# Sparse graph attention on 16 graphs: a longer lead of the later projections, two products held back, and no output product in the last places

## The chip, the cores and the metric

The kernel runs on one core of a Trainium2 chip. The metric is the device time of one execution in microseconds (us), the median of several runs. Engines are called PE (TensorE matmul; PEld is its weight load), DVE (VectorE), ACT (ScalarE), POOL (GpSimd) and SP (SyncE, which here only issues DMAs).

## The reference

The input x is 16 batches of 1024 nodes with 512 features (float32), adj a 1024 x 1024 matrix of zeros and ones that all batches share; it is sparse, with few ones in most rows and many in the first ones. There are 8 heads of 64 features.

```python
q = (x @ Wq + bq).reshape(b, n, H, HD)        # k, v alike
scores = jnp.einsum('bqhd,bkhd->bhqk', q, k) / jnp.sqrt(jnp.float32(HD))
scores = scores + (1.0 - adj)[None, None, :, :] * -1000000000.0
attn = jax.nn.softmax(scores, axis=-1)
out = jnp.einsum('bhqk,bkhd->bqhd', attn, v).reshape(b, n, d)
layer = out @ Wo + bo
x = _layernorm(x + layer, axis=-1, eps=1e-5)
```

A row of adj without any one attends to all nodes alike, so its result is the mean of v.

## The kernel before, in words

**Data.** The nodes are sorted by degree, and a batch's rows form 8 tiles of 128 queries (NT = 8). Because a query has only a few keys, attention is no dense matmul: for each tile the kernel walks over *blocks*, and a block holds one key for each of the tile's 128 queries. POOL gathers the key and value rows of a block by an indirect DMA (`kvg`, L1242) from a DRAM buffer `kv_pair`, which holds k and v of two batches (the first two batches have buffers of their own, `kv_rows`; PAIRED_FROM = 2). DVE multiplies q by k (`qk`, L1263) and reduces by head (`s`, L1267); ACT takes exponentials (L1278) and weighs v with them (L1291), or DVE does (L1295); DVE adds two weighed blocks (L1307); PE sums them in PSUM (`sum`, L1316 and L1317). After a tile's last block DVE normalises it (`o`, L1329 to L1337), and PE transposes it (`poT`, L1351) for its output product `po` with Wo (L790). A statistic chain over DVE, ACT and POOL (L1100 to L1125; the power at L1113 or L1143 on POOL, the shift at L1116 on DVE) makes the layer norm, and POOL stores the rows (L1125).

**The order of the work.** All engines' instructions are written out in one order (manual schedule). A loop counts *places* n, from -39 to some 540. There are 530 blocks, one per place; batch b begins at place `start[b]`: 0, 34, 68, 100, 134, 166, 200, 232, 266, 298, 332, 364, 398, 430, 464, 496, and 530 is the end. At place n the loop writes the products and scores of block n+4, exponentials of n+3, weighing of n+1 or n+2, the gather of block n+8 (AHEAD; AHEAD_LAST = 11 once no projections are left), and callbacks that earlier places left for this one (`later(k, fn)`: k places on). Then it lets PE do *units* as long as a *credit* lasts, which grows by a share per place: pieces of output products (`finish`, four matmul units and, late in the run, one for the bias), or the next unit of `fronts`, a list with the projections of the batches to come. A function put into `urgent` goes as well (the transposes `turn`, and `mean_pe`).

**Fronts.** For each pair of tiles (`pair`) these are: the transposes of x (`transpose_x`, pxT L748), q (pq, L790), and k and v by seven half products (x, p*, z; L947) that DVE and ACT combine (L959 to L980). Each tile's `out` callback starts the load of x three tiles on (`load_x`, for batches above 0 an indirect DMA of POOL, L1001; three buffers), and for tiles in STORED also a store of x as residual (SP). k and v go to DRAM through SP (L840), q as well; after the last pair PE makes the mean of v (pm, L858), whose write (L864) sets `set_up[b]`; only then may gathers of batch b be written. The first gather of an odd batch from 3 on is `more` (L1217): the first tile of two successive batches is worked off together in the odd one.

How many fronts are done in batch b's stretch is set by a lead in places ahead of a batch's start: `ahead = EARLY + FIRST * (1 - max(0, b - 1) / LATE)`, with EARLY = 13, FIRST = 11 and LATE = 12. In the last batches (from 13 on) the share spreads what is left over the places up to `fronts_end`.

**The lead-in.** Before place 0 the kernel also builds the key lists from adj. Those of tile 7 and 6 are built beside the first places (`REST_FROM`), by a generator `edges(t)`: each `yield` in it means one place later. DVE finds the sorted keys (L635 to L669), PE counts the degrees before each query (`poff`, L675), DVE goes on (L677 to L688, `codes`), PE places them (`pe` L698, `pof` L719), and DVE extracts. Another generator, `bias_setup`, makes the bias of the output: PE transposes the bias rows (L408), DVE copies and spreads bv (`bvb`, L415), PE multiplies by Wo (`pb`, L419), DVE adds bo (L421).

**The end.** After the last projection, output products are the only units of PE beside the sums. `finishing` holds the units of the product begun; none is begun in the last two places of 530. Products of some tiles (SPILL) have their transposed inputs stored and are reloaded (`reload`) for this end, named oTs in the profile.

Of the kernel before, what the change touches and what calls it, by code (L numbers as in the profile page):

```python
# [38 lines left out]
PAIRED_FROM, SPARED = 2, 56  # L39
# [9 lines left out]
AHEAD_LAST = 11  # L49

ROWS = 3
EARLY = 13

FIRST = 11
LEAD_IN = 39
FRONT_BY = -14
SEGMENT = 64
# [120 lines left out]
def kernel(  # L178
# [37 lines left out]
    B, N, D = x.shape  # L216
    HD = D // HEADS
    NPAIR = D // P
    NT = N // P
# [28 lines left out]
    def broadcast(t, v):  # L248
        nc.scalar.dma_start(t, bass.AP(tensor=v.tensor, offset=v.offset, ap=[[0, P], [1, D]]))
# [4 lines left out]
    with ExitStack() as main:  # L254
# [6 lines left out]
        def fill_psum(name):  # L261
            return psum.tile([P, HALF], F32, tag="fill", name=name, bufs=4)
# [74 lines left out]
        def merged(b):  # L337
            return b >= PAIRED_FROM and b % 2 == 1
# [55 lines left out]
        def bias_setup():  # L394
            bk_bc = work.tile([P, D], F32, tag="y", name="bk_bc", bufs=Y_BUFS)
            broadcast(bk_bc, bk)
            yield
            n4 = small.tile([P, NPAIR], F32, name="bk_norms", bufs=1)
            nc.vector.tensor_tensor(bk_bc, bk_bc, bk_bc, op=OP.mult)
            nc.vector.tensor_reduce(n4, bk_bc.rearrange("p (h d) -> p h d", d=P), axis=AX.X, op=OP.add)  # L400
            nc.vector.tensor_reduce(bk_norm, n4, axis=AX.X, op=OP.max)
            n8 = small.tile([P, HEADS], F32, name="bq_norms", bufs=1)
            nc.vector.tensor_tensor(bk_bc, bq_bc, bq_bc, op=OP.mult)
            nc.vector.tensor_reduce(n8, bk_bc.rearrange("p (h d) -> p h d", d=HD), axis=AX.X, op=OP.add)
            nc.vector.tensor_reduce(bq_norm, n8, axis=AX.X, op=OP.max)
            yield
            pb = fill_psum("pb")
            nc.tensor.transpose(pb[:, 0:2 * NPAIR], bias_rows, ident[:2 * NPAIR, :2 * NPAIR])  # L408
            nc.tensor.transpose(pb[:, 2 * NPAIR:3 * NPAIR], bv_rows, ident[:NPAIR, :NPAIR])
            yield  # L410
            nc.vector.tensor_copy(bias_qk, pb[:, 0:2 * NPAIR])
            bv_col = one.tile([P, NPAIR], F32, name="bv_col")
            nc.vector.tensor_copy(bv_col, pb[:, 2 * NPAIR:3 * NPAIR])
            bvb = work.tile([P, NPAIR, P], F32, tag="y", name="bvb", bufs=Y_BUFS)
            nc.vector.tensor_copy(bvb, bv_col[:, :, None].to_broadcast([P, NPAIR, P]))  # L415
            yield
            pb = fill_psum("pb3")
            for c in range(NPAIR):
                nc.tensor.matmul(pb, bvb[:, c, :], W["o"][:, c, :], start=(c == 0), stop=(c == NPAIR - 1))  # L419
            yield  # L420
            nc.vector.tensor_tensor(bo_bc, pb, bo_bc, op=OP.add)  # L421
# [18 lines left out]
        now, plan, rest, urgent, known, waiting, combined = [0], {}, {}, [], [], [], []  # L440

        def later(k, fn):
            plan.setdefault(now[0] + k, []).append(fn)
# [187 lines left out]
        def edges(t):  # L631
# [38 lines left out]
                nc.vector.tensor_tensor(check[:, 2 * NT + 1:2 * NT + 2], ranked[:, t, 1:2], st[:, 0:1], op=OP.subtract)  # L670

            nc.vector.tensor_scalar(deg, ranked[:, t, 1:2], -float(K), 0.0, op0=OP.add, op1=OP.max)
            yield
            po = fill_psum(f"poff_{t}")
            nc.tensor.matmul(po[:, 0:1], before, deg, start=True, stop=True)  # L675
            yield
# [15 lines left out]
            for i0 in range(0, nb, step):  # L692
                n = min(step, nb - i0)
# [21 lines left out]
            for i0 in range(0, nb, 4):  # L715
                n = min(4, nb - i0)
# [15 lines left out]
        def load_x(b, t):  # L732
            if b < B:
                if b and not known:
                    waiting.append((b, t))
                    return
                X[b, t] = work.tile([P, D], F32, tag="x", name=f"x_{b}_{t}", bufs=3)
                if b:
                    gather_x(X[b, t], b, t)
                else:  # L740
                    nc.sync.dma_start(X[b, t], x[b, ds(t * P, P), :])

        def transpose_x(b, t):
            def pe():
                xs = X.pop((b, t))
                p = fill_psum(f"pxT_{b}_{t}")
                for c in range(NPAIR):
                    nc.tensor.transpose(p[:, ts(c, P)], xs[:, ts(c, P)], ident)  # L748

                def out():  # L750
                    XT[b, t] = work.tile([P, D], F32, tag="xT", name=f"xT_{b}_{t}", bufs=4)
                    nc.scalar.copy(XT[b, t], p)
                    n = b * NT + t + 3
                    if t == 0 and b >= PAIRED_FROM:
                        if not merged(b):
                            BOTH[b // 2] = work.tile([P, 2, NPAIR, P], F32, tag="place", name=f"both_{b}", bufs=1)
                        nc.scalar.copy(
                            BOTH[b // 2].rearrange("p w c (h n) -> p h c w n", h=2)[:, b % 2],
                            p.rearrange("p (c w n) -> p c w n", c=NPAIR, w=2),
                        )  # L760
                        sq = work.tile([P, D], F32, tag="ysq", name=f"sq_x_{b}", bufs=1)
                        nc.scalar.activation(sq[0:LONE, :], xs[0:LONE, :], AF.Square, accum_out=x_norm[0:LONE, b:b + 1])
                    if b * NT + t in STORED:
                        nc.sync.dma_start(residual[b * NT + t], xs)
                        later(2, lambda: load_x(n // NT, n % NT))
                    else:
                        load_x(n // NT, n % NT)
                    if t % 2 and (b, t) != (0, 1):
                        later(1, combine)

                def combine():
                    s = [work.tile([P, HD2], F32, tag=f"s{i}", name=f"s{i}_{b}_{t}", bufs=1 + i // 4) for i in (1, 2, 3, 4)]
                    x0, x1 = XT[b, t - 1], XT[b, t]
                    nc.vector.tensor_tensor(s[0], x1[:, 0:HD2], x1[:, HD2:D], op=OP.add)
                    nc.vector.tensor_tensor(s[2], x0[:, 0:HD2], x1[:, 0:HD2], op=OP.subtract)
                    nc.vector.tensor_tensor(s[1], s[0], x0[:, 0:HD2], op=OP.subtract)
                    nc.vector.tensor_tensor(s[3], x0[:, HD2:D], s[1], op=OP.subtract)
                    SX[b, t // 2] = s

                later(1, out)  # L780

            return [(TRANSPOSE, pe, lambda: (b, t) in X)]
# [403 lines left out]
        start = [min(n for n, block in enumerate(blocks) if block[0] == b) for b in range(B)] + [len(blocks)]  # L1186
# [245 lines left out]
        done, coming, spilled, gathered, fronts, guarded = [], [], [], [0], [], []  # L1432

        total = len(blocks)
# [19 lines left out]
        for t, n in REST_FROM.items():  # L1454
            prep.setdefault(n, []).append(edges(t))
# [7 lines left out]
        with tc.manual_schedule():  # L1463
# [13 lines left out]
                return fronts_by[b - 1] + (part - int(part)) * (fronts_by[b] - fronts_by[b - 1])  # L1477

            finishing, last_finish, reloads, last_reload = [], -LEAD_IN, 0, 0
            fronts_end = start[B - 1] - 12  # L1480
            credit = 0.0
            for t in range(3):
                load_x(0, t)
            n = -LEAD_IN
            while n < total or plan or rest or urgent or done or finishing or spilled or lone_tiles or not guarded:
# [6 lines left out]
                elif n in start:  # L1492

                    b = start.index(n)
                    left = sum(u[0] for u in fronts)
                    ahead = EARLY + FIRST * (1 - max(0, b - 1) / LATE)
                    goal = fronts_time - needed(b + 2, ahead / NBT)
# [38 lines left out]
                    reload(*spilled.pop(0), reloads)  # L1536
                    reloads, last_reload = reloads + 1, n
                first_unit = True
                while credit > 0 or urgent:
                    if urgent and not (first_unit and fronts):  # L1540
                        urgent.pop(0)()
                        continue
                    if (
                        not finishing and len(done) > (LAZY if fronts else 0) and n > loaded.get(done[0], n) + 1
                        and n > last_finish + bool(fronts) and not total - 2 <= n < total
                    ):
                        finishing = finish(*done.pop(0))
                        last_finish = n
                    units = finishing or fronts
                    if not units:  # L1550
                        if urgent:
                            urgent.pop(0)()
                            continue
                        break
                    cost, fn, ready = units[0]
                    if ready and not ready():
                        if urgent:
                            urgent.pop(0)()
                            continue
                        break  # L1560
                    del units[0]
                    fn()
                    credit -= cost
                    first_unit = False
                credit = min(credit, 2 * share)
# [39 lines left out]
```

## Time and profile before

| What | us |
| --- | --- |
| median of three runs | 1888.14 |
| the three runs | 1887.98, 1894.98, 1888.14 |
| the profiled execution | 1894.52 |
| its span, first to last instruction | 1892.4 |
| PE busy in it, mean granted clock 0.990 | 1816.5 |
| first score reduction (L1267) of batch 12, 13, 14, 15 | 1436.00, 1535.97, 1636.63, 1746.03 |

The profile is one execution; its span is 2.1 us shorter than its time, and its time is 6.4 us above the median. A place takes about 3.1 us (2.96 in batch 13, 3.46 in batch 15). Units of PE by the groups: one matmul of 128x512 about 0.6 us in the records, and as each is pipelined with the next, two of them (the two passes of a float32 product) take 0.86 us of PE in sequence. The groups with the most DVE time are the reduction of scores (681 ns each), the product with q (684 ns) and the addition of two blocks (694 ns); a gather on POOL takes 1131 ns.

### The profile page before, as it was taken

The page shows a single profiled execution, that of the slowest core. Times are in us where ns is not written, and L with a number is a line of the kernel's source. Part 1 is how long each engine was busy: PE and PEld are TensorE (multiplying, and loading weights), DVE is VectorE, ACT ScalarE, POOL GpSimd, SP SyncE. Part 2 cuts the span into 40 slices and gives each one's busy share as a digit, 9 for nine tenths or more (in the row PEclk, how much of TensorE's full clock was granted, in tenths as well). Part 3 has the DMA queues.
Part 4 walks back from the last instruction along what each step waited for, and adds up shares of the span by engine and source line. Part 5 has one row for each costly group of instructions (what it writes and reads, how often), then busy time and mean ns, then how long its engine had stood idle before and what let it go on. Part 6 is the DMA issues. An engine that isn't in the chain of part 4 may idle for free. (4 is left out here: it accounts for less than half of the span.)

```text
span 1892.4 us, 25171 instructions
## 1 busy us (share of the span) xinstructions
PE 1816.5 (96%) x5149; PEld 876.6 (46%) x5149; DVE 1695.3 (90%) x3470; ACT 1557.4 (82%) x6128; POOL 1262.6 (67%) x1189
## 2 busy tenths in 40 slices
PE   7979999999999999999999999999999999999996
PEld 3434444444545454444444444444545444444442
DVE  6888879999998999899999989899999989997875
ACT  3627868988888988988898878988899989977885
POOL 1366765777676776767676766767676866656884
PEclk9989999999999999999999999999999999999998
DMA  7356786888989897989889897989889899989993
GB/s 279 115 167 215 226 290 229 309 298 291 322 266 319 303 333 256 345 290 310 299 284 329 279 324 261 334 303 309 286 302 352 297 332 319 329 282 319 340 332 137
DMA packets 188149, 544.63 MB, mean 288 GB/s; under 512 B 32602, under 2 KB 32622, under 8 KB 187986
## 3 DMA queue, kind: packets, MB, share of 16 engines
q0 software_dynamic: 116400, 382.82, 60.4%
q1 hardware_dynamic: 68510, 154.30, 21.7%
q10 hardware_dynamic: 3076, 5.82, 0.8%
q14 instruction: 120, 0.98, 0.2%
q8 instruction: 43, 0.70, 0.2%
HBM read 419.52 MB, written 144.34 MB: 298 GB/s over the span
## 5 line engine op out<-in xcount | busy, mean ns | idle before, releaser
L1291 ACT ACTIVATE pv<-kvg,pv 128x64 f32<-128x64 f32 x3544 | 893.4, 340 | 1.8 <-issue 1.8
L1242 POOL DMA_INDIRECT kvg<-kv_pair,place_row x462 | 522.6, 1131 | 258.6 <-issue 94.5
L790 PE MATMUL po<-wo,oT 128*128 128x512 f32 x816 | 379.2, 600 | 2.0 <-DVE vsum L854 1.2
L790 PE MATMUL pq<-wq,xT 128*128 128x512 f32 x792 | 369.4, 598 | 1.3 <-DVE s L1267 0.8
L1267 DVE TENSOR_REDUCE s<-qk 128x8 f32<-128x512 f32 x530 | 360.8, 681 | 7.2
L1263 DVE TENSOR_TENSOR qk<-qt,kvg 128x512 f32<-128x512 f32 x434 | 296.8, 684 | 13.2 <-DMA kvg<-kv_pair,place_row 13.1
L947 PE MATMUL x<-b,xT 128*128 128x512 f32 x504 | 239.0, 597 | 0.1
L947 PE MATMUL pp<-t,s 128*128 128x512 f32 x504 | 237.3, 593 | 1.5 <-DVE t L383 1.5
L1307 DVE TENSOR_TENSOR pv<-pv,pv 128x520 f32<-128x520 f32 x329 | 228.4, 694 | 8.2 <-ACT pv L1291 8.0
L790 PEld LDWEIGHTS po<-wo,oT 128*128 128x128 f32 x816 | 153.4, 192 | 171.7 <-issue 162.7
L790 PEld LDWEIGHTS pq<-wq,xT 128*128 128x128 f32 x792 | 149.0, 192 | 169.3 <-issue 157.7
L1001 POOL DMA_INDIRECT x<-in_x_dram,asked_row x120 | 129.6, 1080 | 103.5 <-PE pxT L748 35.4
L1278 ACT ACTIVATE pv<-s,absent 128x8 f32<-128x8 f32 x434 | 126.8, 293 | 55.1 <-DVE s L1267 36.6
L1125 POOL DMA_INDIRECT out_dram<-y,asked_row x129 | 145.1, 1125 | 35.9 <-issue 25.0
L800 ACT ACTIVATE sq_k<-kv 128x128 bf16<-128x128 f32 x512 | 150.8, 300 | 8.4 <-DVE kv L970 4.5
L947 PEld LDWEIGHTS x<-b,xT 128*128 128x128 f32 x504 | 95.3, 192 | 111.6 <-issue 105.2
L947 PEld LDWEIGHTS pp<-t,s 128*128 128x128 f32 x504 | 94.1, 190 | 111.3 <-issue 102.2
L947 PE MATMUL z<-b,s 128*128 128x512 f32 x252 | 121.4, 604 | 13.1 <-DVE kv L975 10.4
L1196 POOL DMA_INDIRECT qg<-q_rows,query_row x96 | 105.5, 1099 | 28.5 <-issue 25.3
L1029 POOL DMA_INDIRECT y<-in_x_dram,asked_row x93 | 105.0, 1129 | 26.1 <-issue 25.8
L947 PE MATMUL z<-t,s 128*128 128x512 f32 x252 | 118.6, 593 | 0.0
L947 PE MATMUL pp<-t,xT 128*128 128x512 f32 x252 | 118.5, 592 | 0.0
(276 smaller groups left out, 2750.2 us busy)
## 6 DMA issues: line engine op xcount, KB each, us to landing
kv_pair<-kv SPq DMA_DIRECT2D x98, 512.0 KB
q_rows<-q SPq DMA_DIRECT2D x106, 256.0 KB
qt<-q_rows SPq DMA_DIRECT2D x98, 256.0 KB
residual<-x SPq DMA_DIRECT2D x36, 256.0 KB
y<-residual SPq DMA_DIRECT2D x36, 256.0 KB
kv_rows<-kv SPq DMA_DIRECT2D x15, 512.0 KB
kvg<-kv_pair,place_row POOLq DMA_INDIRECT x462
kv_pair<-kv SPq DMA_DIRECT2D x28, 256.0 KB
```

The lines of the kernel that those rows point to most:

```text
L790: nc.tensor.matmul(p, lhs(c), w[:, c, :], start=(c == 0), stop=(c == NPAIR - 1))
L800: nc.scalar.activation(sq, s[:, ts(h, P)], AF.Square, scale=scale, accum_out=sums[:, h:h + 1])
L947: nc.tensor.matmul(R[bank], l[:, ts(c, P)], right[:, c, :], start=(first and c == 0), stop=(c == 1), skip_group_check=True,)
L1001: nc.gpsimd.indirect_dma_start(out=y, out_offset=None, in_=x_rows, in_offset=bass.IndirectOffsetOnAxis(ap=asked_row[:, t:t + 1], axis=0), ...
L1125: nc.gpsimd.indirect_dma_start(out=out_rows[b, t], out_offset=bass.IndirectOffsetOnAxis(ap=rows, axis=0), in_=y, in_offset=None, element_o ...
L1196: nc.gpsimd.indirect_dma_start(out=q, out_offset=None, in_=q_rows[b % ROWS], in_offset=bass.IndirectOffsetOnAxis(ap=rows, axis=0))
L1242: nc.gpsimd.indirect_dma_start(out=KG[n], out_offset=None, in_=rows, in_offset=bass.IndirectOffsetOnAxis(ap=(place_row if b else key_row)[ ...
L1263: nc.vector.tensor_tensor(QK[n], q, KG[n][:, 0:D], op=OP.mult)
L1267: nc.vector.tensor_reduce(S[n], QK.pop(n).rearrange("p (h d) -> p h d", d=HD), axis=AX.X, op=OP.add)
L1278: nc.scalar.activation(PV[n][:, D:], S.pop(n), AF.Exp, bias=bias)
L1291: nc.scalar.activation(pv[:, ts(h, HD)], v[:, ds(D + h * HD, HD)], AF.Copy, scale=pv[:, D + h:D + h + 1])
L1307: nc.vector.tensor_tensor(PV[b, t], PV[b, t], pv, op=OP.add)
```

## The change

It has four parts, all in the order of the work; no instruction is added to or taken from a projection, an attention block or an output product.

- **Held back:** in `edges` and in `bias_setup`, three yields instead of one stand ahead of the products poff and pb, so these are written two places later.
- **Lead:** EARLY becomes 17 and FIRST 7 (their sum stays 24), and `fronts_end` is 16 places ahead of the last batch's start instead of 12.
- **Loads of x:** the load that a tile's `out` starts comes 4 places later instead of 2 for tiles in STORED, and 2 places later instead of at once for the first tile of batches from PAIRED_FROM on.
- **Last places:** in places 527, 528 and 529 no unit of an output product or projection is written; before, only the beginning of a product was excluded, in the places 528 and 529.

```diff
-EARLY = 13
-FIRST = 11
+EARLY = 17
+FIRST = 7
...
             nc.vector.tensor_copy(bvb, bv_col[:, :, None].to_broadcast([P, NPAIR, P]))
-            yield
+            for _ in range(3):
+                yield
             pb = fill_psum("pb3")
...
             nc.vector.tensor_scalar(deg, ranked[:, t, 1:2], -float(K), 0.0, op0=OP.add, op1=OP.max)
-            yield
+            for _ in range(3):
+                yield
             po = fill_psum(f"poff_{t}")
...
                     if b * NT + t in STORED:
                         nc.sync.dma_start(residual[b * NT + t], xs)
+                        later(4, lambda: load_x(n // NT, n % NT))
+                    elif t == 0 and b >= PAIRED_FROM:
                         later(2, lambda: load_x(n // NT, n % NT))
                     else:
                         load_x(n // NT, n % NT)
...
-            fronts_end = start[B - 1] - 12
+            fronts_end = start[B - 1] - 16
...
-                while credit > 0 or urgent:
+                last_sums = total - 3 <= n < total
+                while credit > 0 and not last_sums or urgent:
...
-                    units = finishing or fronts
+                    units = [] if last_sums else finishing or fronts
```

## The prediction

> **What bounds the kernel now.** I read the page's first part (busy time of each engine), then the groups with what ended the idle time before them, then the timeline of PE and DVE around each place that the diff touches, and last the table of windows. The chain of waits helps less: PE has only 28% of it, in pieces of many lines.
>
> ```profile
> PE 1816.5 (96%) x5149; PEld 876.6 (46%) x5149; DVE 1695.3 (90%) x3470; ACT 1557.4 (82%) x6128; POOL 1262.6 (67%) x1189
> ```
>
> PE is busy for 1816.5 of 1892.4 us, so all its idle time is 75.9 us. DVE stands close behind at 90%. No edit takes a matmul away, so the change can win only out of those 75.9 us and out of stretches where PE runs at half clock. From the timeline: the lead-in (the first 160 us) holds the larger waits (7.42, 2.19, 1.20, and the first loads, which no edit touches); from 160 to 1740 us there are some 31 us in 28 small waits; the rest is the tail.
>
> ```profile
> 108.23 0.38 PE L675 MATMUL poff<-est,before 128*128 128x1 f32 x2 [2.19 <-DVE est L669]
> 109.75 1.86 PE L858 MATMUL pm<-vsum,mean 128*1 128x512 f32 x2
> ...
> 136.40 5.44 PE L419 MATMUL pb<-wo,bvb 128*128 128x512 f32 x8 [7.42 <-DVE bvb L415]
> ...
> 157.25 1.98 PE L947 MATMUL z<-b,s 128*128 128x512 f32 x4 [1.20 <-DVE kv L975]
> ```
>
> The columns are start, duration, engine, line, operation; the bracket is the idle time before and its releaser. These are the two products whose yields the diff lengthens: the list offsets (poff) waited 2.19 us and the bias product (pb) 7.42 us, each for a DVE result that DVE had just been given.
>
> At the other end of the run, batch 13 begins at about 1536 us:
>
> ```profile
> 1526.75 1.96 POOL L1217 DMA_INDIRECT more<-kv_pair,place_row  x1 [4.95 <-issue]
> ...
> 1538.72 0.69 DVE L1263 TENSOR_TENSOR qk<-qt,kvg 128x512 f32<-128x512 f32 x1 [1.47 <-DMA kvg<-kv_pair,place_row]
> 1543.34 0.69 DVE L1263 TENSOR_TENSOR qk<-qt,kvg 128x512 f32<-128x512 f32 x1 [1.53 <-DMA kvg<-kv_pair,place_row]
> ...
> 1558.81 0.66 PE L1351 MATMUL poT<-ident,o 128*128 128x128 f32 x4 [1.63 <-DVE o L1337]
> 1565.36 0.66 PE L1351 MATMUL poT<-ident,o 128*128 128x128 f32 x4 [2.46 <-DVE o L1337]
> ```
>
> POOL's first gather of the batch stood 4.95 us before it could start, the gathers behind it came late, DVE waited 1.47 and 1.53 us for them, and PE then waited for DVE.
>
> ```profile
> 109.20:112.60 3.40, 3.40 (x5) 0.63 (x5) 3.30 (x13) 0.57 (x1) 0.00 (x0) 0.50 0.56 189
> 136.40:139.90 3.50, 3.50 (x4) 1.51 (x5) 3.43 (x7) 1.21 (x5) 2.89 (x3) 0.50 0.51 164
> 1535.97:1636.63 100.66, 93.33 (x270) 44.65 (x269) 94.27 (x180) 89.93 (x372) 66.13 (x62) 0.98 0.90 311
> 1846.00:1869.30 23.30, 21.42 (x56) 10.51 (x54) 18.53 (x53) 19.50 (x60) 14.37 (x16) 0.93 0.53 187
> ```
>
> Columns: window, length, busy time (count) of PE, PEld, DVE, ACT and POOL, granted clock, DMA share, GB/s. After the 2.19 and the 7.42 us waits PE ran 3.4 to 3.5 us at clock 0.50. Batch 13's 34 blocks took 100.66 us, of which PE worked 93.33 and DVE 94.27.
>
> **What the skill says of it.** The Trainium skill, "TensorE: Matmul & The Clock Gate", section "Part 1: The HAM clock gate", says that an idle TensorE falls to half clock, judged over windows of about 3.4 us, and advises against gaps of over about 3 us. The trace has the half clock for about that long, but after waits from 1.73 us on, and none after 1.63 us or less. I go by the trace: a wait of 1.7 us or more costs 3.4 / 2 = 1.7 us on top. The same skill's "DMA: Bandwidth & Descriptors", section "Rules for kernel authors", says that a DMA which reads what another wrote has to be held until that one's completion semaphore. The trace agrees: the held gather (4.95 us) reads kv_pair, whose last writes SP issued from 1522.68 to 1527.24. An earlier write is therefore the right lever there.
>
> **The change part by part.** The profiled execution took 1894.52 us (span 1892.4), 6.38 above the median of 1888.14. I sum against 1894.52 and then take 6.38 off.
>
> *A: three yields instead of one ahead of poff and pb.* The instruction order shows no new instruction; products move two places back. For the list of tile 7, PE's next instruction is then pq (no wait, two units), then pm, which needs vsum: DVE finishes that at 109.62, in order behind est, where pm now starts at 109.75. So the 2.19 us just move to pm: gain 0. DVE now waits for pp before g some 4.55 instead of 2.67 us, and its 2.1 us of list work (L677 to L688) go behind g. So DVE finishes bvb at about 137.9 instead of 136.15. PE meanwhile does six units that stood behind pb (two each of pq, x, pp, 6 x 0.86 = 5.2 us, from 128.8 to 133.95), and waits 137.9 - 133.95 = 4.0 instead of 7.42. That still costs the half clock, as before. DVE then sets the pace: transposes wait for a bank (about 1.3), poff for g (about 1.7), and z behind kv (L975) begins at 154.4 instead of 157.25: -2.85. The list's other products now come 0.35 later: **-2.5**. Bounds: -9 if nearly all of both waits goes (2.19 + 7.42 = 9.6), +1 if DVE's added wait of 1.9 us is passed on.
>
> *B: the lead.* With EARLY 17 and FIRST 7 the lead of the projections (13 + 11 places at batches 0 and 1, both 24 in sum) falls more slowly: for b = 12 it is 17 + 7/12 = 17.6 instead of 13.9 places, and the last projection is due at place 480 instead of 484. The instruction order has the batch's last mean (pm) at 14 places ahead of its start instead of 10 (batch 13), 9 (14 and 15); the gathers still run 8 ahead. Four places at 3 us are 12 us, over the 4.95, so POOL's wait goes. The writes of k and v move on SP's queue past some four q reads of 0.3 us (L1229), which have their places of slack; cost 0. What it cost: DVE 1.47 + 1.53 + 0.43 and 2.24 for a statistic of POOL's behind the same queue, 5.7 in sum; PE 0.66 + 1.63 + 2.46 = 4.75, with a half clock 6.4. DVE works 94.27 of the 100.66 us there, so at most 6.4 can go; I take 5. Batch 15's first gather also waited (2.86), but PE has some 3.8 us of work per place there and hides it: 0. Next late: the x of batch 14, tile 5 is loaded one place before its transpose (three or more elsewhere; four in the middle of the run before); a gather of 1.1 us and its landing within some 3 us: 0 to 3 us and a half clock, I take 1.5. Sum **-3.5** (bounds -6.4 and 0). Projections done earlier also leave output products for later; as PE does both, this is a swap, cost 0 while PE is bound.
>
> *C: loads of x two places later (also the first tile of each batch from 2 on).* One POOL DMA each (1.08 us, L1001), moved, none added. In the order each x still has three places or more but the one above. The moved gathers pass kvg gathers on POOL's queue, which is 67% busy; SP's stores keep their places. **0**, with -6 to +6 for the small waits of mid-run, whose order shifts by a few places: some 20 us of them come from PE and DVE handing over, and nothing here takes that away.
>
> *D: no product in places 527 to 529.* In the order the four products that stood behind place 522 (4 x 3.65 = 14.6 us) come before it: the last is at 521 instead of 527, since B's earlier projections also leave places for them. PE's end then: the sums and products up to the last sum ended at 1869.30; without the four sums of 522 to 528 (4 x 0.86) the last product ends at 1865.9, less the idle that it fills: 1.88 and its half clock 1.7 at 1849.40, and half of 4.0 (1.15 + 1.13 + 0.82 + 0.90, PE's waits from 1730 to 1824): 5.6, so 1860.3. Behind it DVE has y (0.7), the four 0.61 us operations of place 523 (2.45), two of 524 with statistics (1.6), four of 525 (2.45) and two of y (1.3); ACT weighs 529 (1.9) behind that, done at about +10; add, sum, and the four operations to o end at +12.7: 1873.0. Before, o was ready at 1871.66. **+1** (bounds -3 and +5: 12.7 may be 10 if ACT hides, or 2.5 more if a statistic waits for POOL). What follows (the last tile's transposes, product, norm, store) is the same.
>
> Sum: -2.5 - 3.5 + 0 + 1 = -5: 1889.5, less 6.38: **1883**.
>
> **The rivals.**
> 1. *All the waits go*: lead-in -9, batch 13 -6.4, tail -3 make -18.4: 1870. For it: each wait named has its cause moved. Against: DVE is 90% busy and the releaser of most of them.
> 2. *The change does not do what it says*: DVE sets the pace at each place, the waits move to the next instruction (as poff to pm): 0, 1888.
> 3. *Slower: the tail loses its cover.* From place 522 PE has only sums, and DVE, ACT and POOL run in series. A shift on DVE waiting for POOL's power (2.46 at 1840.87 and 4.23 at 1845.32 before, with PE products beside them) would stand in the open: 6.7, and with D's own 12.7 against a gain of only 3.6 (half of 4.0 not filled: +2) and +1.7 for a half clock this is +10.4; against it A and B at their poorer -6 leave +4.4: 1893. It decides if such a power reaches DVE more than 6 us late behind place 522; otherwise D stays at +1.
>
> **How the numbers follow.** Forecast (1883; own range 1878 to 1888) 0.40; all waits go (1870; 1866 to 1877) 0.22; nothing (1888; 1886 to 1891) 0.20; tail (1893; 1890 to 1901) 0.18. The range, 1868 to 1895, leaves out about a quarter of rival 1 and a third of rival 3 and little else. A change of over 0.5% (9.4 us), about the least that can be told from none here, means below 1878.7 or above 1897.6. Faster: rival 1 and a fifth of the forecast, 0.30; slower: half of rival 3, 0.09; same: 0.61.
>
> **What would show it.** A: the wait before the bias product near 4 instead of 7.42, and pm waiting for vsum where poff waited. B: no wait before the gather "more" of batch 13, and batch 13's DVE waits on kvg gone; the transposes of batch 14's tile 5 waiting for a DMA of x if the short lead hurts. C: as many small waits from 160 to 1740 us, about 31 us. D: the last four sums without products between them, each behind DVE's pv, with PE idle. I am wrong if the lead-in's z pass does not come about 2.5 us earlier, if batch 13 does not shorten, or if the middle, where I put nothing, moves by more than 6.

## The result

The changed kernel is slower: 1918.27 us median of six runs (1909.17 to 1921.01) against 1895.13 for the kernel before on the same occasions; the ratio is 1.011, with a 95% interval of 1.0077 to 1.0142. The forecast was 1883, taken from 1888.14, so 5 us faster; measured are 23 us slower. The profiled execution of the changed kernel took 1909.17 us (span 1907.3), 14.65 more than that of before; it is the fastest of the six, so it shows less than the whole loss.

The first part of its page answers to the line shown ahead of the forecast:

```profile
span 1907.3 us, 25167 instructions
PE 1821.0 (95%) x5150; PEld 878.4 (46%) x5150; DVE 1694.1 (89%) x3469; ACT 1557.7 (82%) x6128; POOL 1268.4 (67%) x1189
```

PE's idle time rose from 75.9 to 86.3 us, and its busy time by 4.5 with the same matmuls; the other engines' work is the same. By stage, adding PE's waits of 0.3 us or more in the timeline of each kernel: up to 160 us they fell from 23.1 to 20.7; from 160 to 1760 us they rose from 30.7 to 37.2; behind 1760 us from 7.5 to 13.0. So the lead-in's idle time fell by 2.4 us, about what was expected, and the middle, where the forecast put nothing, and the tail lost more.

The timeline of PE in the lead-in (start, duration, instruction, and the idle time before it with its releaser):

```profile
109.81 1.87 PE L862 MATMUL pm<-vsum,mean 128*1 128x512 f32 x2 [2.70 <-DVE vsum L858]
...
140.91 6.60 PE L420 MATMUL pb<-wo,bvb 128*128 128x512 f32 x8 [4.83 <-DVE bvb L415]
147.35 1.04 PE L750 MATMUL pxT<-ident,x 128*128 128x128 f32 x8
149.31 0.38 PE L677 MATMUL poff<-est,before 128*128 128x1 f32 x2 [0.92 <-DVE g L970]
```

The wait of poff went over to pm, which waits for vsum (2.70), and pb waits 4.83 instead of 7.42. But pb itself then took 6.60 instead of 5.44 us, more of it at half clock.

POOL's timeline at the start of batch 13 shows that the gather `more` no longer waits:

```profile
1538.56 0.86 POOL L1221 DMA_INDIRECT more<-kv_pair,place_row  x1 [0.31 <-issue]
```

It waited 4.95 us before. DVE's waits for gathered keys between 650 and 1760 us fell from 14.3 to 4.8 us. So the lead does what it is for. What it brought instead stands in PE's timeline of the middle:

```profile
665.31 3.53 PE L951 MATMUL z<-b,s 128*128 128x512 f32 x4 [4.27 <-DVE kv L979]
...
1424.93 3.78 PE L951 MATMUL z<-b,s 128*128 128x512 f32 x4 [3.75 <-DVE kv L979]
```

At 1533.52 the same line waited 2.04 us more, and at 1624.09 pm waited 3.13 us for vsum. The kernel before had two such waits over 2 us, 2.67 at 876.73 and 3.86 at 1097.85. In this pair of profiles the waits of this kind (0.3 us or more, between 160 and 1760 us) add up to 13.0 us against 9.2, so they are 4 of the 6.5 us that PE's waits rose there. Why DVE was late is told by its own timeline ahead of the first one (PE's first z pass ended at 659.3):

```profile
659.96 0.69 DVE L1103 TENSOR_TENSOR y<-po,y 128x512 f32<-128x512 f32 x1
660.68 0.69 DVE L1104 SCALAR_TENSOR_TENSOR y<-bo_bc,y 128x512 f32<-128x512 f32 x1
661.30 0.08 DVE L1104 DVE_READ_ACCUMULATOR y<-bo_bc,y 128x1 f32 x1
661.30 0.69 DVE L1267 TENSOR_TENSOR qk<-qt,kvg 128x512 f32<-128x512 f32 x1
661.90 0.69 DVE L1311 TENSOR_TENSOR pv<-pv,pv 128x520 f32<-128x520 f32 x1
662.51 0.68 DVE L1271 TENSOR_REDUCE s<-qk 128x8 f32<-128x512 f32 x1
663.11 0.41 DVE L778 TENSOR_TENSOR s<-xT 128x256 f32<-128x256 f32 x1
...
664.57 0.68 DVE L979 TENSOR_TENSOR kv<-z,g 128x512 f32<-128x512 f32 x1
```

DVE was not idle for a moment. z has one PSUM bank. The first z pass fills it, DVE reads it (v of the pair's second tile, L979; called *the z reader* below), and only then may the second z pass add to it. In between PE normally has q of the second tile (3.4 us) and the pass p4 (1.7 us). In the first pair of every batch from 1 on that q is left out, because tile 1 is the tile of single keys, and only p4 covers the read. Here the reader stood behind an output row (y, 1.3 us), the block's own three operations (1.8) and the four sums of x (1.4), 4.6 us from 659.96 to 664.57. PE stood still for 4.27 us, and then ran at half clock (3.53 us for what takes 1.88). Which rows and sums fall into the place of the reader is settled by how many places ahead each batch's projections run, and this is what the lead changes. **Theory K** says that the cost is such a coincidence in DVE's queue. It has two rivals: the tail pays (**T**, the uncovered last sums), or DVE's sheer amount of work at that lead sets the pace (**W**, and then it doesn't matter in which order DVE does it). Ahead of the first runs K was called M, the loss in the middle by whatever order.

The last sums behave as forecast, without a product between them (PE's timeline again):

```profile
1875.59 0.70 PE L1320 MATMUL sum<-pv,sums 128*128 128x256 f32 x2 [1.12 <-DVE pv L1299]
...
1879.52 0.70 PE L1320 MATMUL sum<-pv,sums 128*128 128x256 f32 x2 [2.78 <-DVE pv L1299]
...
1882.74 1.22 PE L1320 MATMUL sum<-pv,sums 128*128 128x256 f32 x2 [2.08 <-DVE pv L1299]
```

### The profile page after: what moved, and what is told of

It is laid out like the page before. It is cut to its first block, busy times and chain, and to the rows that moved or that the text cites. A ratio compares the mean times of both kernels' runs of the same rounds, so it can differ in the third digit from the quotient of the medians.

```text
span 1907.3 us, 25167 instructions
## 1 busy us (share of the span) xinstructions
PE 1821.0 (95%) x5150; PEld 878.4 (46%) x5150; DVE 1694.1 (89%) x3469; ACT 1557.7 (82%) x6128; POOL 1268.4 (67%) x1189
## 5 line engine op out<-in xcount | busy, mean ns | idle before, releaser
L1129 POOL DMA_INDIRECT out_dram<-y,asked_row x129 | 152.0, 1179 | 37.1 <-issue 25.1
```

Source lines behind the costliest of these rows:

```text
L1129: nc.gpsimd.indirect_dma_start(out=out_rows[b, t], out_offset=bass.IndirectOffsetOnAxis(ap=rows, axis=0), in_=y, in_offset=None, element_o ...
```

## The experiments

All were compared with the kernel before on the same chip. The kernel before took 1877 us on three chips, 1898 and 1909 on two others; so kernels that ran on one chip are compared first, and those of different chips with reserve. How much reserve is needed can be seen below: e7 and e15 are one and the same kernel, and their ratios to before are 1.0031 on the chip of 1909 us and 1.0071 on one of 1877 us, with intervals that do not meet.

### Each part alone

`e1_yields` has only the three yields, `e2_lead` only the lines below, `e3_loads` only the loads of x, `e4_last` only the last places.

```diff
-EARLY = 13
-FIRST = 11
+EARLY = 17
+FIRST = 7
...
-            fronts_end = start[B - 1] - 12
+            fronts_end = start[B - 1] - 16
```

> Only the two products held back (three yields), all else as before. Both theories: the lead-in gains 2.5 us (the idle time before 160 us is 23.1 before and 20.7 with the whole change), the rest stays; 2 to 3 us faster than before. If places behind the lead-in shift by more than 3 us against before, a small shift of the order's timing alone costs time in the middle, and neither theory is complete.

> Only EARLY 17, FIRST 7 and fronts_end 16 places ahead. Theory M (the middle pays: with another lead projections and attention meet in another order on PE and DVE from place 68 to 430): 10 to 15 us slower than before, lost between 500 and 1450 us, in waits of PE for DVE of 1 to 4 us with half clock behind the long ones. Theory T (the tail pays, since no product covers the last places): within 3 us of before.

> Only the later loads of x (4 instead of 2 places for stored tiles, 2 instead of 0 for the first tile from batch 2 on). Theory M as stated puts the loss on the lead: here within 3 us of before. A rival to it (theory L: x arrives late, or the moved gathers hold up the gathers of keys on POOL): 7 us or more slower. Theory T: within 3 us.

> Only no unit of a product in places 527 to 529. Theory T: 8 us or more slower, with PE idle before each of the last sums (the whole change has 2.4 to 3.3 us there, 11.7 in sum, with half clock). Theory M: 0 to 5 us slower, since without the earlier projections only the product of places 527 has to go elsewhere (3.65 us behind the last sum, in the open).

Measured, as ratio to before with its interval: e1 0.9997 (0.9989 to 1.0006), e2 **1.0109** (1.0095 to 1.0123), e3 1.0009 (1.0002 to 1.0016), e4 1.0004 (0.9996 to 1.0013). The lead alone is the whole loss, some 20 us; the three other parts, each measured alone, add up to 2 us. T in the form "the last places cost it" falls. The yields missed: 2 to 3 us were expected, none came.

e4's profile, equal to before in time, serves as before on that chip. Against it, e2's waits of PE for the z reader are these:

```profile
660.54 3.78 PE L947 MATMUL z<-b,s 128*128 128x512 f32 x4 [4.14 <-DVE kv L975]
...
1416.38 3.29 PE L947 MATMUL z<-b,s 128*128 128x512 f32 x4 [3.75 <-DVE kv L975]
```

with a third of 3.16 at 1523.81. e4 has one, 3.86 at 1081.34. Spans differ by 26.0 us (1900.4 and 1874.4). PE's waits of 0.2 us or more are longer by 4.7 us between 160 and 1760 us (30.3 and 25.6) and by 4.6 behind that (11.8 and 7.2). The time given up to a lower clock, added over windows of 5 us as (1 - granted clock) x 5, is 31.6 us in e2 and 13.6 in e4: 18.0 more, 10.3 of them between 160 and 1760 us. Part of the tail's share falls into idle time, so the whole sum counts a few us twice; but in the middle, of this pair, the half clock (10.3) is more than the added waits (4.7). For the z reader alone the waits there are 14.5 us against 8.2, and five stretches of 3.41 us at half clock follow them against one: 6.3 + 6.8, or 13 of the 26 us. The pair of before and after is different: there the clock given up between 160 and 1760 us is 6.8 us in both, so that in those two profiles the middle lost by waiting alone.

### The lead's two halves, and the reader first

`e5_curve` changes only EARLY and FIRST, `e6_end` only fronts_end. `e7_lead_v1` is the lead with the reader at the head of its place, `e8_v1` is the kernel before with the same edit:

```diff
-                    later(1, after)
+                    if after is out_v1:
+                        at = plan.setdefault(now[0] + 1, [])
+                        at.insert(at.index(out_g) + 1 if out_g in at else 0, after)
+                    else:
+                        later(1, after)
```

> Only EARLY 17 and FIRST 7; the last projection stays due 12 places ahead of the last batch. Theory K (the new lead makes places in which DVE has an output row, the sums of x and v of the same pair in one queue, so that PE waits 3 to 4 us for the read of its z bank, with half clock behind): 12 to 16 us slower than before, that is the middle's share of the lead's 20. Rival E (the earlier end of the projections costs it all, by a tail without products): within 3 us.

> Only the due time of the last projection, 16 places ahead instead of 12. Theory K: 4 to 8 us slower, all of it behind 1800 us, where the products end earlier and the last sums wait for DVE with PE idle. Rival E: 15 to 20 us slower.

> The new lead, with one change in DVE's order: the addition that reads the z bank (v of the pair's second tile) is put at the head of its place's callbacks, or straight behind the addition that makes g where that is in the same place, instead of behind the output rows and sums of x. Theory K: the three waits of PE for it of 3.2 to 4.1 us fall below 1.5, with the half clock behind them: 7 to 12 us faster than the new lead alone, so 8 to 13 us slower than before. If DVE's amount of work sets the pace (rival W), the waits move elsewhere: within 3 us of the lead alone, 20 slower than before.

> The kernel before with the same change in DVE's order. Theory K: its one long wait (3.86 with 1.7 of half clock) and some of 1.2 to 1.4 go: 4 to 8 us faster. Rival W: within 2 us.

Measured on a chip where before took 1909.37: e5 1.0072 (1.0042 to 1.0103), e6 1.0014 (0.9997 to 1.0031), e7 1.0031 (1.0015 to 1.0047), e8 0.9977 (0.9962 to 0.9992). The curve of the lead carries most of the loss (13.7 us, as K expected), its end 2.7 us with an interval from -0.6 to 5.9 (below the middle of the 4 to 8 expected by K). The reader first gains with the new lead and a little with the old one, as K expected of both: e8 is 4.4 us **faster than the kernel before** (1.5 to 7.3). The lead with its end was not run without the reader first on this chip.

### Output rows last, and other leads

`e9_lead_rows` (new lead) and `e10_rows` (kernel before) write the output rows' additions last in their place (`later_last` instead of `later` for the callback of po). `e11_half` has EARLY 15, FIRST 9 and 14 places at the end, `e12_more` EARLY 19, FIRST 5 and 16.

> The new lead, with the two DVE additions of each output row written behind the other work of their place instead of among it. In the order this takes them from in front of the z reader in batch 13 (batch 14 keeps a pair, of means; batch 6 has the four sums of x). Theory K: every hand-off of DVE to PE (z, sums of v, q) is earlier, 5 to 12 us faster than the lead alone, so 8 to 15 us slower than before. Rival W (DVE's amount of work sets the pace): within 3 us of the lead alone.

> The kernel before with the output rows' additions written last in their place. Theory K: the wait of batch 10 (3.86) falls below 2; 2 to 6 us faster, unless the rows, now later, hold up the output products' bank. Rival W: within 2 us.

> Half of the lead's change: EARLY 15, FIRST 9, end 14 places ahead. Rival S (a longer lead costs by its length, by whatever it takes from the batch in hand): half of the lead's 20, some 10 us slower. Theory K: what counts is how often the z reader has output rows or sums of x ahead of it: the order has that in batch 11 (sums of x behind two normalised tiles) and 15, so one long wait in batch 11 and 0 to 6 us slower.

> One and a half times the lead's change: EARLY 19, FIRST 5, end 16 places ahead. Rival S: some 28 us slower. Theory K: the order has output rows ahead of the z reader in batches 6 and 7, and sums of x in 11 and 14: long waits of PE there, none in batch 13, 12 to 22 us slower, about the lead's own loss and no more.

Measured: e9 1.0181 (1.0168 to 1.0195), e10 1.0051 (1.0038 to 1.0064), e11 1.0033 (1.0022 to 1.0044), e12 1.0045 (1.0028 to 1.0063).

Putting all rows last was a miss: with either lead the kernel is slower for it. Rows are not in the way in general; K holds at most for the z reader. The two other leads speak against a cost of the lead's length: half the change costs 5.7 us, the change 20 to 23 (on two other chips on which the kernel before took 1877 us), one and a half times the change of EARLY and FIRST, with the same end, 7.6. In e11 the long wait stood where the order of instructions had put it, in batch 11:

```profile
1191.74 3.78 PE L947 MATMUL z<-b,s 128*128 128x512 f32 x4 [4.80 <-DVE kv L975]
```

In e12 it didn't: the order had named batches 6, 7, 11 and 14, and the waits came in batches 4 (4.10) and 8 (2.42). Counting what stands ahead of the reader in its own place is thus a poor forecast of a single wait, since DVE may come to that place early or late; and 12 to 22 us were expected of e12, not 8.

### The lead, the nudge and the reader first on one chip

`e13_lead_2` is e2 again and `e15_lead_v1_2` e7 again, `e16_after_v1` the whole change with the reader first, and `e14_nudged` the lead with

```diff
-                    ahead = EARLY + FIRST * (1 - max(0, b - 1) / LATE)
+                    ahead = EARLY + FIRST * (1 - max(0, b - 1) / LATE) + {4: -0.6, 11: 1.2, 12: -1.5}.get(b, 0.0)
```

> The new lead alone, again, as the measure for the three kernels beside it on the same chip. Both theories: 17 to 23 us slower than before, with PE's waits of 4.1, 3.8 and 3.2 us for the z reader in batches 6, 13 and 14.

> The new lead, with 0.6 places less while batch 4 runs, 1.2 more in batch 11 and 1.5 less in batch 12, picked from the order of instructions so that no output row and no sums of x stand ahead of the z reader in batches 6 and 13 (batch 14 keeps its pair of rows). Theory K: the waits of 4.1 and 3.8 us fall below 1.5 and the half clock behind them goes, (4.1 + 3.8 - 2 x 1) + 2 x 1.7 = 9: 6 to 12 us faster than the lead alone. Rival W (DVE's amount of work at that lead): within 3 us of the lead alone.

> The new lead with the z reader at the head of its place, on the same chip as the lead alone. Theory K: 7 to 14 us faster than the lead alone. Rival W: within 3 us of it.

> The whole change with the z reader at the head of its place. Theory K: as with the lead alone, 7 to 14 us faster than the whole change (which is 1.1%, some 21 us, slower than before), so 6 to 14 us slower than before. Rival W: still 18 us or more slower than before.

Measured: e13 1.0124 (1.0109 to 1.0139), e14 1.0096 (1.0082 to 1.0110), e15 1.0071 (1.0058 to 1.0083), e16 1.0072 (1.0057 to 1.0087). With the reader first the lead is 0.5% faster than without, about 10 us of the 23 (1.0124 - 1.0071, times 1877); the whole change then costs 0.72% instead of 1.1%, though the latter is of another chip. W, which allowed 3 us, falls. Not all of the 10 us is cost of the lead, as the same edit took 4.4 us off the kernel before (e8). The edit halves the waits rather than ends them; e15's timeline of DVE shows why, beside PE's line:

```profile
1409.65 2.86 PE L947 MATMUL z<-b,s 128*128 128x512 f32 x4 [2.41 <-DVE kv L979]
```

```profile
1405.63 0.42 DVE L774 TENSOR_TENSOR s<-xT 128x256 f32<-128x256 f32 x1 [3.67 <-PE z L947]
...
1408.91 0.68 DVE L979 TENSOR_TENSOR kv<-z,g 128x512 f32<-128x512 f32 x1
1409.51 0.68 DVE L1103 TENSOR_TENSOR y<-po,y 128x512 f32<-128x512 f32 x1
1410.22 0.69 DVE L1104 SCALAR_TENSOR_TENSOR y<-bo_bc,y 128x512 f32<-128x512 f32 x1
```

The reader (L979) now goes ahead of the two rows, and the 1.33 us they took ahead of it come off the wait (3.74 in e13). The sums of x and the block's own three operations are still in front of it. And DVE had stood idle for 3.67 us just before: the first of those sums waited for PE's first z pass, which ended at 1405.52 (in e13 the same wait was 3.68). Each of the two engines waits for the other in turn, so neither is busy all the time. Putting the sums behind the reader was not tried.

The nudge gained 0.28%, 5 us, less than the 6 to 12 expected and more than W's 3: by time alone it is inconclusive. By place it is clearer. Batch 15 began at 1748.5 us instead of 1758.9 in e13 (first score reduction), with the same projections done by then; then the tail gave half of it back: PE's waits behind 1760 us rose from 12.8 to 17.0 us, with these two at their head:

```profile
1850.10 1.07 PE L1316 MATMUL sum<-pv,sums 128*128 128x256 f32 x2 [4.66 <-DVE pv L1295]
...
1874.57 1.09 PE L1351 MATMUL poT<-ident,o 128*128 128x128 f32 x4 [5.83 <-DVE ends L1345]
```

So a shift of at most one and a half places in three batches moved the middle by 10 us one way and the tail by 5 the other.

### Is the half clock a cost of its own?

`e17_lead_warm` puts three products of W and the identity, which nobody reads, ahead of the second z pass of the first pair of batches 6, 13 and 14. `e18_v1_yields` is e8 with the yields of the change.

> The new lead, and three products whose result nobody reads (0.86 us each, 2.6 in sum) on PE ahead of the second z pass of the first pair in batches 6, 13 and 14; DVE's, ACT's, POOL's and SP's orders are the same. They lie in waits of 4.1, 3.7 and 3.0 us and leave 1.5, 1.1 and 0.4 idle. If the half clock behind a long wait is a cost of its own (1.7 us each): 4 to 6 us faster than the lead alone, so 17 to 19 us slower than before, and the clock stays at 1.00 there. If it isn't, or the fill holds PE up: no faster than the lead alone.

> The kernel before with the z reader at the head of its place and the two products of the lead-in held back. Theory K: 3 to 6 us faster than before (4.4 with the reader first alone, and the held-back products changed nothing by themselves). Rival W: within 2 us.

Measured on a chip where before took 1898.06: e17 1.0064 (1.0042 to 1.0086), e18 0.9987 (0.9968 to 1.0005). In e17 the fill stands where it was meant to, and the z pass runs at full speed behind it. The table of windows from 1433.29 on gives clock 1.00 (columns as ahead of the forecast), where e13 had 0.57 behind the same wait unfilled:

```profile
1429.38 2.74 PE L999 MATMUL warm<-wq,ident 128*128 128x512 f32 x6
1433.29 1.98 PE L947 MATMUL z<-b,s 128*128 128x512 f32 x4 [1.17 <-issue]
```

```profile
1433.29:1436.80 3.51, 3.51 (x8) 1.62 (x9) 3.44 (x9) 1.83 (x8) 2.60 (x4) 1.00 0.74 239
```

```profile
1412.57:1416.31 3.74, 0.00 (x0) 0.00 (x1) 3.71 (x8) 3.74 (x18) 2.82 (x4) 1.00 0.89 317
1416.31:1419.80 3.49, 3.49 (x5) 1.65 (x6) 3.42 (x9) 2.00 (x9) 2.58 (x4) 0.57 0.73 215
```

Behind the two other fills the clock stayed at 1.00 as well. The kernel is 12 us slower than before where the lead alone was 20 to 23 slower, but the lead alone wasn't run on that chip, and e7 and e15 show that one kernel's ratio can differ by 0.4% (some 8 us) between chips. So the runs don't show that the fill gained time; that the half clock costs time is worked out from the traces' clock, and no run isolates it. e18 can't be told from before: 2.5 us faster (-0.9 to 6.1). As it contains e8's edit, and the yields alone gave nothing, it is a weak second measure of e8, whose gain of 0.23% thus rests on one chip.

## Why the prediction was wrong, step by step

- **A, the lead-in (-2.5).** The mechanism came as told: poff's wait moved to pm at no gain, pb's wait fell to 4.83 (4.0 forecast), poff waits for g (0.92; 1.7 forecast). The size was off: the z pass behind kv began at 156.50 instead of 157.25, 0.75 us earlier and not 2.85, since pb's own product lengthened by 1.2 us at half clock. Alone the yields gave a ratio of 0.9997: zero within 2 us. Even the fall of pb's wait is not theirs for certain: without them it was 6.91 us in e3 and 5.28 in e4, and the idle time up to 160 us was 20.1 and 19.3 there, 19.5 with them (e1).
- **B, the wait ahead of batch 13 (-3.5).** It went, as did DVE's waits for keys; batch 14's tile 5 did not wait for its x. The 34 blocks took 98.90 us (1555.29 to 1654.19) instead of 100.66: -1.8 for the 5 forecast. (SP's writes "from 1522.68 to 1527.24" can't all have held the gather, which started at 1526.75; the write of the mean at 1522.68 is the one that it needs in the kernel's order.)
- **B, the rest: here it failed.** "as PE does both, this is a swap, cost 0 while PE is bound", and, under C, for the waits of mid-run "0, with -6 to +6". The amount of work stayed the same, but the swap wasn't free. PE is bound only on average; at each hand-off with DVE either may have to wait. The new lead put other work of DVE's in front of the read of z. In place of 0 the lead measured +20 to +23 us alone (e2, e13). Writing the z reader first takes 10 of them away (e15); as it also took 4.4 off the kernel before (e8), 6 to 10 us of the loss go through the z reader. Rival 3, the slower one, looked for the loss in the tail, and its 1893 with a range up to 1901 was too low. (Its +10.4 leaves out D's own +1, and the -6 that it calls the poorer A and B is the forecast's own -2.5 - 3.5.)
- **C, the loads of x (0).** e3 measured 1.0009 (1.0002 to 1.0016), 1.7 us: right, if at the edge.
- **D, the last places (+1).** Alone 1.0004, 0.8 us. The picture forecast for the tail, sums without products and each behind DVE, came; but the tail's added 5.5 us of idle time come with the lead: e4, which has D alone, has 7.2 us of waits there, as before, and e2, without D, 11.8. Of the lead's two halves it is the earlier end that adds it: 13.3 us in e6, 8.2 in e5.
- **The half clock.** The forecast took "a wait of 1.7 us or more costs 3.4 / 2 = 1.7 us on top" as a rule. In e5 a wait of 3.75 us, the same as e13's above, had none behind it:

```profile
1431.50:1435.25 3.75, 0.00 (x1) 0.00 (x1) 3.71 (x8) 3.75 (x21) 2.94 (x3) 1.00 0.64 172
1435.25:1438.75 3.50, 3.50 (x8) 1.63 (x9) 3.43 (x9) 3.50 (x17) 2.59 (x4) 1.00 0.75 259
```

The Trainium skill's page "TensorE: Matmul & The Clock Gate", section "Part 1: The HAM clock gate", says that the window in which idleness is judged runs freely (the advice against gaps of over about 3 us that the forecast puts there stands further on, in "Why this matters for your kernels"); that agrees with this pair, in which one and the same wait once costs 1.5 us of clock and once nothing. The traces show the windows themselves: within a run, the stretches at half clock start at whole multiples of 3.413 us from one another (in the changed kernel's at 665.60 and 1423.36, 222 of them apart). Cut along these windows, e13's wait falls mostly into one, e5's into two (first two lines e13, then e5):

```profile
1413.40:1416.81 3.41, 0.50 (x1) 0.30 (x2) 3.38 (x7) 3.41 (x16) 2.49 (x4) 1.00 0.87 291
1416.81:1420.22 3.41, 3.41 (x5) 1.35 (x4) 3.34 (x9) 1.50 (x6) 2.80 (x3) 0.50 0.76 238
1430.09:1433.50 3.41, 1.41 (x4) 0.34 (x2) 3.38 (x8) 3.41 (x19) 2.20 (x3) 1.00 0.53 174
1433.50:1436.91 3.41, 1.66 (x4) 0.87 (x5) 3.34 (x8) 3.41 (x17) 2.63 (x3) 1.00 0.83 245
```

PE was idle for 2.91 us of e13's window, and the next one ran at 0.50; in e5 it was idle for 2.00 and 1.75, and neither was followed by it. Counted so over the twenty traces (from 160 us to 30 us before the end, windows at full clock), each of the 69 windows with over 2.0 us of idle time was followed by half clock, none with under 1.77 was, and between these some were. So the forecast's 3.4 us stands, and its threshold belongs to a window's idle time and not to a single wait. What a wait costs is partly luck: the three long waits of the z reader, 4.14, 3.75 and 3.2 us in both, have five such windows behind them in e2 and one in e5.

**What stays open.** Of some 23 us 6 to 10 are the z reader with its half clock, and the end of the projections is 2.7 us with an interval from -0.6 to 5.9. The remaining 10 to 14 lie, as far as is known, in other hand-offs that the traces show (pm for vsum 3.1, a sum for pv 2.9, in some runs a reload of a spilled tile 4.1 us), none of which was taken away by itself. That each is a coincidence of the same kind, and not a cost of this lead by itself, is argued from e11 and e12, not shown.

## What to carry to other kernels

Where two engines, each busy about 90% or more, hand work to each other in a written-out order, a change that only shifts work between stages is not neutral: look up, at each tight hand-off (a single bank, a short cover), what the new order puts ahead of the reader. When a knob like a lead is judged, try its neighbours too: 15/9 and 19/5 cost 6 and 8 us, 17/7 between them 20. And try putting the reader that another engine waits for at the head of its place; that gained 10 us with the new lead, and 4.4 with the old one on the one chip where it was clear of noise, while moving all rows to the end lost with both.

## What was unexpected of the hardware

The same program differs by chip: the kernel before took 1877 us on three chips, 1898 and 1909 on two, and nearly all its runs lay within 5 to 7 us on each of the first and within 18 to 22 on the others. And two profiles of the same loss can split it differently: in e2 against e4 the middle gave up 10.3 us of clock and 4.7 of waits, in after against before no clock and 6.5 us of waits.
